# A second output row of the 3x3 convolution completed by accumulating transfers

## The chip, the cores and the metric

The kernel runs on one core of a Trainium2 chip. The metric is the device time of one execution in microseconds (us). Profiles are of one execution; a line L*n* is line *n* of the kernel before.

## The reference

Two bottleneck blocks follow each other on x of shape (64, 1024, 14, 14), float32. Each block is a 1x1 convolution to 256 channels, a 3x3 convolution from 256 to 256 channels with padding 1, and a 1x1 convolution back to 1024. Every convolution is followed by a batch normalization over images and pixels, and the first two also by a ReLU. The result is scaled by a softplus of one parameter, added to x and rectified:

```python
out = relu(bn(conv(x, w1, b1, 1, 0), g1, be1))
out = relu(bn(conv(out, w2, b2, 1, 1), g2, be2))
out = bn(conv(out, w3, b3, 1, 0), g3, be3)
return relu(x + softplus(residual_scale)[0] * out)
```

## The kernel before, in words

The 256 middle channels lie as two slots of 128 partitions in one tile `y` that stays in on-chip memory for the whole run. The stage of this change is the 3x3 convolution, `conv2`, once in each layer (from 305 to about 580 us and from 1276 to about 1560 us of the profile). It replaces `y` in place by the convolution of `y`, in eight groups `g` of eight images.

Along the rows a fast convolution with four output rows per tile and six products is used. For each group VectorE and ScalarE make six combinations of the input rows, in three pairs, (1, 2), (3, 4) and (5, 0) (`combine`). Products 3 and 4 have three row tiles (168 columns in a matmul), the others four (224). Each pair goes into tiles `r`, `v`, `sums` and `diffs` (`Inputs`). Along the columns there is a second fast scheme: TensorE makes for each product the parts `m` (from `sums`), `l` (from `diffs`) and `columns` (from `v`). ScalarE copies `m` into the two `columns` banks (L758, L760) and `l` to `ls` (L768). VectorE adds banks and `ls` into a tile `f` (L801, called from `outputs`). `f` has three buffers in turn, `columns` and `ls` two and three; the transformed filters of each product come by two loads on SP's queue (`ua`, `ub`, L651), which wait until TensorE has read the buffers.

`finish` turns the six products of a group, in the order in which they are made, into output rows. `out_rows[k]` are the rows k, k+4, ... of the 14. From the first two `f` it makes `a` and `d` (L829, L830: tiles `fa` and `fb` in the profile), from the next two `c` and `e` (L835, L836). Rows 1 and 2 are then written with L593 (the line of the helper `stt`). Row 0 lacks the sixth product, and row 3 and the last row (row 13, named `end`) lack the fifth. In the groups 0 to 5 (`by_transfer`) row 0 is begun by VectorE (L843) and ScalarE (L844), and completed by two transfers that add the sixth `f` to it (L871, GpSimd's queue). In the groups 6 and 7 VectorE completes it. Row 3 and `end` are completed by VectorE in all groups, in L859 and L860, from `d3` (the first three tiles of `d`, updated by L847 through the helper at L593) and the fifth `f`.

ScalarE also computes the statistics of the group before in four passes (`moment`, L900), which read all of that group's `y`, beside products 2 to 5 of a group, and normalizes the group that follows (`norm`) beside products 0 and 1.

On TensorE the order is written out in the loop at the end of `conv2`: `l` of product k, half of its `columns`, `m` of product k+1, the other half. On VectorE and ScalarE a scheduler orders the instructions, except where `keep_in_program_order` fixes them. All instructions of one engine start in order.

Of the kernel before, what the change touches and what calls it, by code (L numbers as in the profile page):

```python
# [38 lines left out]
AF = mybir.ActivationFunctionType  # L39
ALU = mybir.AluOpType  # L40

P = 128
N, C, H, W = 64, 1024, 14, 14
# [3 lines left out]
MS = M // P  # L47
# [40 lines left out]
def bottlenecks(ctx: ExitStack, tc: tile.TileContext, x, w1s, w2s, w3s, pars, out):  # L88
    nc = tc.nc
# [6 lines left out]
    y_grp = y_all.rearrange("p s (g h l) -> p s g h l", g=NG, h=H)  # L96
# [459 lines left out]
    def conv2(psum, pool, b, par, aff, affine_of, stats):  # L556
# [14 lines left out]
        full = RT - 1  # L571
# [12 lines left out]
        def new(tag, tiles=RT):  # L584
            v = pool.tile([P, MS * RT * LINE], FP, tag=tag, name=tag, bufs=BUFS.get(tag, 1))
            return v[:, : MS * tiles * LINE].rearrange("p (s r l) -> p s r l", s=MS, r=tiles)
# [5 lines left out]
        def stt(to, a, by, c):  # L592
            return nc.vector.scalar_tensor_tensor(to, a, by, c, ALU.mult, ALU.add)  # L593
# [210 lines left out]
        def halves(f):  # L804

            return f.rearrange("p o r (i q c) -> p q (o r i) c", i=GI, q=2)

        def outputs(c):
            return c.add_to(new("f", c.lines // GI))

        def finish():


            for g in range(NG):
                out_rows = [y_grp[:, :, g, k::4, :] for k in range(4)]
                last_group = g == NG - 1

                by_transfer = g < NG - 2

                def stat(k, lines):  # L820
                    if last_group:
                        for o in range(MS):
                            nc.vector.bn_stats(stats[:, o, 1 + k, :], lines[o])

                ca = yield
                fa = outputs(ca)
                fb = outputs((yield))
                a, d = new("fa"), new("fb")
                nc.vector.tensor_add(a, fa, fb)  # L829
                nc.vector.tensor_sub(d, fa, fb)  # L830

                fa = outputs((yield))
                fb = outputs((yield))
                c, e = new("fc", full), fa
                nc.vector.tensor_add(c, fa, fb)  # L835
                nc.vector.tensor_sub(e, fa, fb)  # L836
                a3, d3 = (v[:, :, :full] for v in (a, d))
                for o in range(MS):
                    stt(out_rows[1][:, o, :full], e[:, o], 2.0, d3[:, o])
                    stt(out_rows[2][:, o], c[:, o], 4.0, a3[:, o])  # L840
                if by_transfer:

                    nc.vector.tensor_add(out_rows[0][:, :, :full], a3, c)  # L843
                    nc.scalar.activation(out_rows[0][:, :, full], a[:, :, full], AF.Copy)  # L844
                else:
                    nc.vector.tensor_add(a3, a3, c)
                stt(d3, e, 8.0, d3)  # L847
                if g == 0:
                    begin(out_rows[1][:, :, :full])
                if last_group:  # L850
                    for o in range(MS):
                        lines = y_grp[:, o, g, 1 : 1 + 4 * full].rearrange("p (r k) l -> p r k l", k=4)[:, :, :2]
                        for k in range(2):
                            moment(lines, idle[:, : 2 * full * LINE].rearrange("p (r k l) -> p r k l", k=2, l=LINE), o, k, g)

                fa = outputs((yield))

                end = y_grp[:, :, g, H - 1]
                nc.vector.tensor_add(out_rows[3], d3, fa[:, :, :full])  # L859
                nc.vector.tensor_add(end, d[:, :, full], fa[:, :, full])  # L860
                stat(0, [out_rows[3][:, o] for o in range(MS)])
                stat(1, [end[:, o] for o in range(MS)])
                if last_group:
                    merge()

                cb = yield
                if by_transfer:

                    f = outputs(cb)
                    for o in range(MS):  # L870
                        nc.gpsimd.dma_start(out=out_rows[0][:, o], in_=f[:, o], accum_op=ALU.add)  # L871
                    continue
                nc.vector.tensor_add(halves(a), halves(a), cb.by_columns(cb.ls))
                for j, q in enumerate((EVEN, ODD)):
                    for o in range(MS):
                        to, more = (
                            v[:, o].rearrange("p r (i q c) -> p q r i c", i=GI, q=2)[:, q] for v in (out_rows[0], a)
                        )
                        nc.vector.tensor_add(to, cb.banks[:, q, o].rearrange("p (r i c) -> p r i c", r=RT, c=WH), more)
                    stat(2 + j, [out_rows[0][:, o].rearrange("p r (i q c) -> p q r i c", i=GI, q=2)[:, q] for o in range(MS)])  # L880
            yield
# [8 lines left out]
        def begin(lines):  # L890

            mv = small.tile([P, MS, nc.vector.BN_AGGR_DIM], FP, tag="mv_first", name="mv_first")
            for o in range(MS):
                nc.vector.bn_stats(first_stats[:, o], lines[:, o])
            for o in range(MS):
                nc.vector.bn_aggr(mv[:, o, :], first_stats[:, o])
            nc.vector.tensor_scalar(center, mv[:, :, 0], -1.0, None, ALU.mult)

        def moment(y, to, o, k, g):
            act(to, y, (AF.Identity, AF.Square)[k], bias=center[:, o : o + 1], accum_out=moments[:, o, k, g : g + 1])  # L900

        def merge():

            n = GPX * (NG - 1) + 2 * full * LINE
            m = small.tile([P, MS, 2], FP, tag="m12", name="m12")
            for o in range(MS):
                nc.vector.tensor_reduce(m[:, o], moments[:, o], mybir.AxisListType.X, ALU.add)
            eng = nc.gpsimd
            eng.tensor_scalar(m, m, 1.0 / n, None, ALU.mult)
            var = small.tile([P, MS], FP, tag="m12var", name="m12var")  # L910
            eng.tensor_tensor(var, m[:, :, 0], m[:, :, 0], ALU.mult)
            eng.tensor_sub(var, m[:, :, 1], var)
            eng.tensor_sub(m[:, :, 0], m[:, :, 0], center)

            for half in range(2):
                to = stats[:, :, 0, 3 * half : 3 * half + 3]
                eng.memset(to[:, :, 0], n / 2)
                eng.tensor_copy(to[:, :, 1], m[:, :, 0])
                eng.tensor_scalar(to[:, :, 2], var, n / 2, None, ALU.mult)
# [26 lines left out]


        made, finished = items(), finish()
        next(finished)
        queue = [next(made) for i in range(3)]  # L950
# [498 lines left out]
```

## Time and profile before

| what | value |
|---|---|
| median of 3 runs | 1959.65 us (1957.53 to 1960.48) |
| the profiled execution | 1959.24 us, span 1957.5 us |
| TensorE matmul / VectorE / ScalarE / GpSimd, busy share of the span | 98% / 79% / 53% / 27% |
| 3x3 convolution, 415 to 449 us (one group): PE / DVE / ACT / POOL busy | 33.67 / 33.35 / 24.98 / 2.55 us of 34.00 |
| DMA share there | 0.70 |
| L859, L860 (16 of each) | 847 and 381 ns |
| L871 (24) | 1262 to 1873 ns on GpSimd, 4.2 to 8.9 us to landing, median 6.5 |
| L844 (12) | 396 ns on ScalarE |

Busy times of VectorE and ScalarE overlap a little from one instruction to the next, so that in a dense stretch the start-to-start time is what counts (a VectorE instruction of 847 ns is followed after 770 ns). The DMA share is the mean busy share of 16 DMA engines.

### The profile page before, as it was taken

Reading aid. Unit: us, or ns where it says so; the run is one execution under the profiler, and the core shown is the slowest. Engines: PE = TensorE matmul, PEld = TensorE weight load, DVE = VectorE, ACT = ScalarE, POOL = GpSimd, SP = SyncE. Lnnn points to the kernel's source line nnn. Section 1 sums busy time; section 2 is a strip of 40 time slices with the busy share of each in tenths; the row PEclk is TensorE's granted clock in tenths of the full one; section 3 lists DMA queues with packets and bytes.
Section 4 is the critical chain, followed back from the end, with each engine's and each line's share of the span. In section 5 each row is a group of like instructions: output and inputs, shape, how many; then the busy total and the mean of one; then the engine's idle time right before and its main releaser. Section 6 shows DMA issues by size and latency. Waiting matters only on the chain.

```text
span 1957.5 us, 26989 instructions
## 1 busy us (share of the span) xinstructions
PE 1919.9 (98%) x9430; PEld 1614.4 (82%) x9430; DVE 1552.4 (79%) x2491; ACT 1041.5 (53%) x2082; POOL 532.0 (27%) x638
## 2 busy tenths in 40 slices
PE   9999999999999999999999999989999999999998
PEld 5555558999997799999999999989999887555554
DVE  5778768999998667676776776699999976888786
ACT  2222214677775055555555555457777641666665
POOL 0111100000105133433433333301010051666664
PEclk9999999999999999999999999999999999999999
DMA  7766635576747634444444444257667386899997
GB/s 289 278 248 254 249 112 165 178 208 191 207 142 203 198 135 187 173 165 177 182 169 165 179 184 166 99 183 204 203 192 207 124 199 232 298 322 339 336 341 264
DMA packets 188983, 408.39 MB, mean 209 GB/s; under 512 B 24944, under 2 KB 165136, under 8 KB 172336
## 3 DMA queue, kind: packets, MB, share of 16 engines
q1 hardware_dynamic: 161728, 324.66, 48.5%
q0 software_dynamic: 21504, 30.94, 6.9%
q10 hardware_dynamic: 5616, 51.06, 6.3%
q8 instruction: 75, 1.23, 0.3%
q14 instruction: 60, 0.49, 0.1%
HBM read 263.75 MB, written 115.34 MB: 194 GB/s over the span
## 4 chain that ended last, share of the span: by engine, by line
PE 90%; DVE 7%; issue 1%; ACT 1%; DMA 1%; SPq 0%; POOL 0%; DVEq 0%
PE ay L168 17%; PE cy L168 16%; PE columns L168 13%; PE cp L168 12%; PE ap L168 10%; PE m L168 6%; PE l L168 6%; PE ax L168 4%; PE cx L168 4%; PE ps L168 1%; DVE x L466 1%; DVE ct L431 1%; DVE f L801 0%; DMA home<-y 0%; DVE ct L433 0%
## 5 line engine op out<-in xcount | busy, mean ns | idle before, releaser
L333 ACT ACTIVATE cu<-cy,scale 128x196 f32<-128x196 f32 (+1 forms) x552 | 257.7, 473 | 286.7 <-PE cy L168 279.6
L168 PE MATMUL columns<-v,ub 128*128 128x224 f32 (+1 forms) x1536 | 301.1, 337 | 0.7 <-ACT columns L760 0.7
L168 PEld LDWEIGHTS columns<-v,ub 128*128 128x128 f32 x1536 | 269.4, 188 | 4.1 <-ACT columns L760 1.2
L333 ACT ACTIVATE x<-x,shift 128x392 f32<-128x392 f32 x428 | 239.7, 613 | 55.1 <-POOL x L492 53.2
L466 DVE SCALAR_TENSOR_TENSOR x<-cp,scale,x 128x196 f32<-128x196 f32 (+1 forms) x368 | 178.1, 484 | 98.0 <-PE cp L168 96.4
L168 PE MATMUL cy<-ct,ws 128*128 128x196 f32 (+1 forms) x736 | 222.0, 383 | 1.1 <-ACT cu L333 1.1
L168 PE MATMUL ay<-at,ws 128*128 128x196 f32 (+1 forms) x752 | 209.2, 381 | 0.0
L487 POOL TENSOR_TENSOR x<-x,cu 128x196 f32<-128x196 f32 (+1 forms) x184 | 159.2, 865 | 174.1 <-ACT cu L333 162.5
L492 POOL TENSOR_TENSOR x<-x,cu 128x392 f32<-128x392 f32 x124 | 125.9, 1015 | 192.8 <-DVE x L466 188.1
L168 PEld LDWEIGHTS ay<-at,ws 128*128 128x128 f32 x752 | 136.4, 190 | 33.6 <-ACT au L333 0.5
L168 PEld LDWEIGHTS cy<-ct,ws 128*128 128x128 f32 x736 | 133.4, 190 | 36.4 <-ACT cu L333 3.8
L168 PE MATMUL m<-sums,ua 128*128 128x224 f32 (+1 forms) x752 | 147.6, 340 | 6.2 <-DVE sums L624 6.2
L168 PE MATMUL l<-diffs,ub 128*128 128x224 f32 (+1 forms) x768 | 149.7, 338 | 3.0 <-PE columns L168 2.9
L513 POOL TENSOR_TENSOR x<-x,cu 128x392 f32<-128x392 f32 x120 | 124.5, 1038 | 86.1 <-DVE x L466 79.2
L871 POOL DMA_DIRECT2D y<-f x24 | 31.1, 1532 | 412.8 <-DVE f L801 320.8
L168 PEld LDWEIGHTS l<-diffs,ub 128*128 128x128 f32 x768 | 133.6, 189 | 7.0 <-PE columns L168 5.9
L168 PEld LDWEIGHTS m<-sums,ua 128*128 128x128 f32 x752 | 132.2, 191 | 8.7 <-DVE sums L624 7.9
L466 DVE SCALAR_TENSOR_TENSOR x<-cx,scale,x 128x196 f32<-128x196 f32 (+1 forms) x184 | 89.3, 485 | 59.1 <-PE cx L168 58.2
L333 ACT ACTIVATE au<-ay 128x196 f32<-128x196 f32 (+1 forms) x141 | 53.6, 380 | 152.0 <-PE ay L168 149.3
L168 PE MATMUL cx<-y,w 128*128 128x196 f32 (+1 forms) x404 | 124.1, 392 | 0.4 <-DVE x L1130 0.4
L168 PE MATMUL cy<-y,w 128*128 128x196 f32 (+1 forms) x404 | 123.8, 392 | 0.0
L168 PE MATMUL cp<-zt 128*128 128x257 f32 x392 | 118.8, 385 | 1.8 <-DVE zt L1030 1.7
(211 smaller groups left out, 3950.1 us busy)
## 6 DMA issues: line engine op xcount, KB each, us to landing
x<-in_x SPq DMA_DIRECT2D x62, 1568.0 KB, 6.8
ub<-u SPq DMA_DIRECT2D x94, 768.0 KB, 5.0
x<-mid SPq DMA_DIRECT2D x32, 1568.0 KB, 8.6
mid<-x ACTq DMA_DIRECT2D x31, 1568.0 KB, 5.1
out<-x SPq DMA_DIRECT2D x123, 392.0 KB, 6.5
ua<-u SPq DMA_DIRECT2D x94, 256.0 KB, 3.0
u<-y POOLq DMA_DIRECT2D x48, 256.0 KB, 5.9
home<-y SPq DMA_DIRECT2D x90, 96.0 KB, 4.2
```

The source lines that it names most:

```text
L168: tc.keep_in_program_order(nc.tensor.matmul(*args, **kw))
L333: tc.keep_in_program_order(nc.scalar.activation(*args, **kw))
L431: nc.vector.tensor_add(t2, t3, ys[0][0])
L466: nc.vector.scalar_tensor_tensor(v, bank, self.scale[:, o : o + 1], v, ALU.mult, ALU.add)
L487: nc.gpsimd.tensor_add(self.part(1, 1), self.part(1, 1), u3)
L492: nc.gpsimd.tensor_add(v, v, self.u12)
L513: nc.gpsimd.tensor_add(v, v, self.u12[:, i * self.n : (i + 1) * self.n])
L871: nc.gpsimd.dma_start(out=out_rows[0][:, o], in_=f[:, o], accum_op=ALU.add)
```

## The change

In the groups 0 to 5 of each layer, row 3 and `end` are completed by transfers with addition too. The update of `d3` now writes its result to row 3 of `y` instead of back to `d3`, in two instructions, one for each slot. ScalarE copies the last tile of `d` to `end`. When the fifth `f` is made, GpSimd's queue issues three transfers that add it to row 3 (one for each slot) and to `end`. L859 and L860 are run in the groups 6 and 7 alone.

```diff
-                stt(d3, e, 8.0, d3)
+                end = y_grp[:, :, g, H - 1]
+                if by_transfer:
+
+                    for o in range(MS):
+                        stt(out_rows[3][:, o], e[:, o], 8.0, d3[:, o])
+                    nc.scalar.activation(end, d[:, :, full], AF.Copy)
+                else:
+                    stt(d3, e, 8.0, d3)
...
                 fa = outputs((yield))
 
-                end = y_grp[:, :, g, H - 1]
-                nc.vector.tensor_add(out_rows[3], d3, fa[:, :, :full])
-                nc.vector.tensor_add(end, d[:, :, full], fa[:, :, full])
+                if by_transfer:
+                    for o in range(MS):
+                        nc.gpsimd.dma_start(out=out_rows[3][:, o], in_=fa[:, o, :full], accum_op=ALU.add)
+                    nc.gpsimd.dma_start(out=end, in_=fa[:, :, full], accum_op=ALU.add)
+                else:
+                    nc.vector.tensor_add(out_rows[3], d3, fa[:, :, :full])
+                    nc.vector.tensor_add(end, d[:, :, full], fa[:, :, full])
                 stat(0, [out_rows[3][:, o] for o in range(MS)])
```

## The prediction

> **What bounds the kernel now.** I read the page's busy shares first, then the busy time by stretch of one convolution group, then the instruction timeline of VectorE and TensorE at the changed place, then the waits.
>
> ```profile
> PE 1919.9 (98%) x9430; PEld 1614.4 (82%) x9430; DVE 1552.4 (79%) x2491; ACT 1041.5 (53%) x2082; POOL 532.0 (27%) x638
> ```
>
> ```profile
> 415.00:449.00 34.00, 33.67 (x194) 33.14 (x193) 33.35 (x37) 24.98 (x48) 2.55 (x2) 1.00 0.70 198
> ```
>
> The page says 79% for VectorE, an average over stages. In one group of the 3x3 convolution (second fence, the busy times by stretch; columns are stretch, length, busy us of PE, PEld, DVE, ACT, POOL, clock, DMA share, GB/s) VectorE is busy 33.35 of 34.00 us and TensorE 33.67. Both look full, so I ask which waits.
>
> ```profile
> 416.40 1.69 PE L168 MATMUL columns<-v,ub 128*128 128x224 f32 x8
> 418.42 1.75 PE L168 MATMUL l<-diffs,ub 128*128 128x224 f32 x8 [0.33 <-PE columns L168]
> ```
>
> ```profile
> 415.47 0.85 DVE L593 SCALAR_TENSOR_TENSOR fb<-f,fb 128x672 f32<-128x672 f32 x1
> 416.24 1.08 DVE L801 TENSOR_TENSOR f<-columns,ls 128x896 f32<-128x896 f32 x1
> 417.24 1.08 DVE L640 TENSOR_TENSOR diffs<-r 128x896 f32<-128x896 f32 x1
> 418.24 0.85 DVE L859 TENSOR_TENSOR y<-fb,f 128x672 f32<-128x672 f32 x1
> 419.01 0.38 DVE L860 TENSOR_TENSOR y<-fb,f 128x224 f32<-128x224 f32 x1
> 419.31 2.95 DVE L699 TENSOR_TENSOR steps<-y 128x2688 f32<-128x2688 f32 x1
> ```
>
> The first of these is TensorE's timeline, the second VectorE's (start, duration, engine, line). See that the block of eight matmuls at 416.40 is followed 2.02 us later, where its neighbours take 1.53: 0.49 us lost. The next block reads `diffs`, and VectorE finished `diffs` (L640) at 418.32. So TensorE waits for VectorE, once in a group. In the next groups the same instruction (L801 of the fifth product) starts 34.07 us later (450.31) and the `l` block 34.08 later (452.50), with the same loss. In another group the loss sits elsewhere:
>
> ```profile
> 468.96 1.30 PE L168 MATMUL l<-diffs,ub 128*128 128x168 f32 x8
> 470.59 1.42 PE L168 MATMUL columns<-v,ub 128*128 128x168 f32 x8 [0.33 <-ACT columns L760]
> ```
>
> ```profile
> 469.81 0.39 ACT L844 ACTIVATE y<-fa 128x224 f32<-128x224 f32 x1 [0.99 <-DVE fa L829]
> ```
>
> There ScalarE stood on L844, which waited for VectorE's `fa`, and the bank fill behind it came late: 1.63 us instead of 1.15, so 0.48 lost. The period is again 34.07. **VectorE's loop sets the period** (34.07, of which it idles only 0.30, for ScalarE's L715), TensorE needs 34.08 - 0.49 = **33.59**.
>
> **What the Trainium skill says.** *Trace Analysis* (Identifying the Most-Contended Engine) warns that matmul busy time doesn't tell how full TensorE is; the trace agrees: 98% busy, yet blocks stretch to 2.02 us. *DMA: Bandwidth & Descriptors* (SWDGE vs HWDGE vs iDMA) says that accumulating transfers go out from GpSimd alone, and that all issuing engines share 16 DMA engines; the trace shows L871 on the software queue, and a DMA share of 1.10 between 426 and 434 us, where they meet the filter loads. *SBUF — State Buffer* (Who interferes with whom) says that a two-input VectorE add meets only GpSimd reads of SBUF, not descriptor writing; the trace agrees: L593 and L624 keep 0.8 us each while L871 is issued (423.56 to 426.1). *VectorE: DVE Perf Modes* (TRN2 errata) says each VectorE instruction pays a fixed extra, so a split one costs more; here two 128x336 take 0.42 us each start to start, one 128x672 takes 0.77.
>
> **The change, part by part, for one of six groups in each of two layers.**
> VectorE: L859 (0.77 start to start) and L860 (0.30) go: -1.07. The update of `d3` (L847) becomes two halves: 2 x 0.42 - 0.77 = +0.07. Net **-1.00 us**. Its loop falls from 34.07 to about 33.07, below TensorE's 33.59, and TensorE becomes the bound: -0.48 a group. VectorE then runs ahead by about 0.5 us a group.
> ScalarE: one copy of 128x224 more (as L844: 0.30 start to start). ScalarE is busy 25 of 34 us; its copy reads `fb`, ready when L830 is done, well before the fifth product. Hidden by its 9 us of idle time.
> GpSimd: three issues more. L871's take 1.26 to 1.87 us, so about 4.2 us (bounds 3.8 to 5.6); the queue has 2.6 of 34 us busy. They start when the fifth `f` ends (417.32), are out by 421.5, and the sixth `f` ends at 423.26, so the old pair isn't delayed. Nothing else stands on that queue here.
> DMA engines: 384 + 384 + 256 rows of 448 bytes, as many as the pair of L871 (2 x 512). Between 345 and 520 us the software queue took 12.5% of 16 engines for 5280 packets: 66 ns each, 4.3 us per engine for 1024. The share rises from 0.70 to about 0.83. It falls at 418 to 427, where the share is 0.53 and 0.39 (416:422, 422:426), not on the 1.10 after it. SP's filter loads land in 5 us and are asked for two products (11 us) ahead: hidden, even 4.3 us later.
> New waits: the fifth `f` tile was free once L860 had read it. Now its buffer (three in turn) is free when the three transfers land. VectorE's second L801 of the next group takes it at 431.95, 14.6 us after 417.32. The third transfer is issued at 417.3 + 2 x 1.4 = 420.1; with the 6.5 us median of L871 it lands at 426.6, with its longest (8.9) at 429.0. Slack 3 to 5 us. Were it late, L829, L830 and all VectorE work for the next products would queue behind it, and then ScalarE's fills and TensorE. The moments (L900) wait for the same transfers, but read the rows at 435.12, behind the old pair.
> Order: in the built order of the changed kernel, VectorE's `diffs` for the next products stands ahead of the `e`/`y` work, so the wait at 418.42 loses its cause; in four of six groups L844 stands between the two bank fills, the order that lost 0.48 at 470.59. With VectorE ahead by over 0.5 us that wait is covered after one or two groups. TensorE's and SP's orders are unchanged.
>
> **The sum.** Start-to-start excess of TensorE's blocks from the fifth product of group 0 on. Layer 0: 0.50, 0.49, 0.48, 0.45 in the groups changed, 0.49 and 0.64 in the last two. Layer 1: 0.65, 0.30, 0.50, 0.49, 0.44, then 0.73 and 0.74. Changed groups 4.3, last two groups 2.6, together 6.9 us. The two stalls of 2.78 us in group 0 (TensorE waits for `sums`, done before L859 starts) stay, as does 1.6 us at half clock in layer 0. The last two groups keep their VectorE work; five groups x 0.5 us of lead help them, and I take two thirds, 1.7. So -4.3 - 1.7 = **-6.0 us**. The profiled execution took 1959.24 (span 1957.5, 1.7 around it), 0.4 under the median of 1959.65. 1959.24 - 6.0 = **1953.2 us**. All of it would give 1952.3, half 1955.8.
>
> **Rivals.**
> A, the wait is only exchanged: L844 between the fills, or a later `f`, costs TensorE 0.48 in each of eight groups in which VectorE isn't ahead. Then 6.9 - 8 x 0.48 = 3.1 remain: 1956.1. For it: that order lost 0.48 in this trace. Against: it lost it with a VectorE loop of 34.07, and that loop is now 33.07.
> B, **slower: the transfers hold the `f` buffer.** If the third lands later than the 14.6 us, VectorE waits at its second L801 for the excess, twelve times; the 1.00 us saved in its loop pays for the first part. With landings of 15 us from issue (435.1) VectorE waits 3.1 us, its loop is 33.07 + 3.1 = 36.2, and the kernel 12 x 2.1 = 25 us slower: 1984. It decides from a landing 13 us after issue. For it: small rows, a queue shared with 55% of filter loads, five accumulating transfers in a row where there were two. Against: L871's longest landing is 8.9 us, and the new ones fall in the emptier stretch.
> C, nothing gained: TensorE's 33.59 hides a limit of the same size (ScalarE's fills), 1959. Against: ScalarE idles 9 us a group.
>
> **How the numbers follow.** About 0.2% (3.9 us) is what a measurement of this kernel can tell from no change. Forecast 0.70 (1951.5 to 1955.5), A 0.13, C 0.05, B 0.12 (1965 to 1990). Of A a third still passes 0.2%. So faster 0.74, same 0.14, slower 0.12. The range takes in forecast and A and leaves out B and most of C: 1951 to 1958.5.
>
> **What would show it.** Right: L859 and L860 only four times each; TensorE blocks at 1.53 with no 2.02 in the middle groups; period of a group 33.6; VectorE busy about 32.3 of 33.6 with idle time in front of L801 or L593; new transfers landing in 6 to 9 us; DMA share about 0.83. Wrong: VectorE idle in front of L801 put down to DMA, ScalarE waiting at the moments for DMA, TensorE waits on ACT L760 in most groups, or a period still at 34.1.

## The result and the profile after

The changed kernel takes 1952.45 us (median of 6 runs, 1949.66 to 1952.98), the kernel before 1958.63 us (6 runs, 1957.53 to 1960.48). The medians are 6.2 us apart. The recorded ratio is 0.9963 with a 95% interval of 0.9952 to 0.9974, which is 5 to 9 us: a small gain and a real one. Measured once more beside the kernel before (e10 below) the medians were 7.6 us apart and the ratio was 0.9961 (0.9949 to 0.9974). The profiled execution has a span of 1951.0 us, where before had 1957.5.

Profiles of a changed kernel show its own line numbers, which are those of before up to L846. In the changed kernel L867 is the pair of transfers to row 3, L868 the one to the last row, L882 the old pair to row 0 (L871 before), and L852 ScalarE's new copy.

The page's busy shares of the changed kernel hardly move:

```profile
PE 1918.5 (98%) x9430; PEld 1617.1 (83%) x9430; DVE 1541.4 (79%) x2479; ACT 1044.6 (54%) x2094; POOL 577.1 (30%) x674
```

VectorE has lost 11.0 us of busy time and the run 6.5 us of span. GpSimd has 45 us more busy time, and nothing waits for it. The stretch of one group shows the change of regime (stretch, length, busy us of PE, PEld, DVE, ACT, POOL, clock, DMA share, GB/s):

```profile
415.00:448.60 33.60, 33.60 (x194) 33.38 (x194) 32.93 (x37) 25.27 (x49) 6.37 (x5) 1.00 0.83 216
```

TensorE is now busy in all 33.60 us. VectorE has 0.7 us to spare. The DMA share rose from 0.70 to 0.83. Next TensorE's and VectorE's timelines at the changed place of the changed kernel (start, duration, engine, line):

```profile
416.34 1.69 PE L168 MATMUL columns<-v,ub 128*128 128x224 f32 x8
417.87 1.67 PE L168 MATMUL l<-diffs,ub 128*128 128x224 f32 x8
419.38 1.69 PE L168 MATMUL columns<-v,ub 128*128 128x224 f32 x8
```

```profile
415.62 1.08 DVE L801 TENSOR_TENSOR f<-columns,ls 128x896 f32<-128x896 f32 x1
416.62 2.95 DVE L699 TENSOR_TENSOR steps<-y 128x2688 f32<-128x2688 f32 x1
419.48 1.08 DVE L801 TENSOR_TENSOR f<-columns,ls 128x896 f32<-128x896 f32 x1
```

The block that took 2.02 us takes 1.53. Behind the fifth product's L801 the two additions are gone, L699 follows at once. `diffs`, for which TensorE had waited, stands earlier (410.56, not shown); e3 below tells whether this new order makes the gain. The waits of TensorE from 336 to 555 us say the same, first of before, then of the changed kernel (who waited for whom, us in total, times, longest):

```profile
PE m L168 <- DVE sums L624: 2.6, 1, 2.6
PE l L168 <- PE columns L168: 1.2, 4, 0.3
PE columns L168 <- ACT columns L760: 0.3, 1, 0.3
```

```profile
PE m L168 <- DVE sums L624: 2.7, 1, 2.7
```

One wait is left, in group 0, ahead of the new transfers (2.69 us where it was 2.61). VectorE's waits in the same stretch of the changed kernel name no DMA:

```profile
DVE r L593 <- ACT r L715: 3.2, 6, 0.7
DVE f L801 <- PE columns L168: 1.0, 1, 1.0
DVE r L682 <- DVE steps L593: 0.5, 1, 0.5
```

Most of VectorE's spare time comes out as a longer wait for ScalarE's L715, which it already had (1.8 us in the same stretch of before). GpSimd's timeline of the changed kernel shows the five issues of a group:

```profile
417.00 2.57 POOL L867 DMA_DIRECT2D y<-f  x2 [26.75 <-DVE f L801]
418.88 1.92 POOL L868 DMA_DIRECT2D y<-f  x1
420.87 2.57 POOL L882 DMA_DIRECT2D y<-f  x2
```

They leave no gap. The DMA view of 345 to 520 us gives the software queue's share and the median time to landing (KB each, us):

```profile
q0 software_dynamic: 10881, 4.70, 23.9%
...
y<-f POOLq DMA_DIRECT2D x10, 224.0 KB, 7.5
y<-f POOLq DMA_DIRECT2D x12, 168.0 KB, 4.6
y<-f POOLq DMA_DIRECT2D x6, 112.0 KB, 8.0
```

The smallest transfer, to the last row, takes longest to land (8.0): it is the third in line. In e4 below the same transfer is issued alone, and lands in 4.0 us (median). Issued at 418.88 it lands at about 426.9; its `f` is taken by L801 at 430.26. 3.4 us of cover are left.

### The profile page after: what moved, and what is told of

Its sections match the earlier page's. It is cut to its first block, busy times and chain, and to the rows that moved or that the text cites. A ratio compares the mean times of both kernels' runs of the same rounds, so it can differ in the third digit from the quotient of the medians.

```text
span 1951.0 us, 27071 instructions
## 1 busy us (share of the span) xinstructions
PE 1918.5 (98%) x9430; PEld 1617.1 (83%) x9430; DVE 1541.4 (79%) x2479; ACT 1044.6 (54%) x2094; POOL 577.1 (30%) x674
## 4 chain that ended last, share of the span: by engine, by line
PE 88%; DVE 5%; issue 5%; ACT 1%; POOL 1%; DMA 1%; SPq 0%; DVEq 0%; POOLq 0%; ACTq 0%
PE cy L168 16%; PE columns L168 14%; PE ay L168 14%; PE cp L168 12%; PE ap L168 9%; PE l L168 7%; PE m L168 7%; PE cx L168 4%; PE ax L168 4%; PE ps L168 1%; DVE x L466 1%; POOL u L215 1%; DVE ct L431 1%; DMA u<-y 0%; DVE ct L433 0%
## 5 line engine op out<-in xcount | busy, mean ns | idle before, releaser
L867 POOL DMA_DIRECT2D y<-f x24 | 30.9, 1529 | 349.5 <-DVE f L801 309.0
```

The lines of the kernel that those rows point to most:

```text
L867: nc.gpsimd.dma_start(out=out_rows[3][:, o], in_=fa[:, o, :full], accum_op=ALU.add)
```

## The experiments

The theory is that VectorE's loop per group sets the period as long as it exceeds TensorE's own need, 33.5 us, and that beyond this point less VectorE work gains nothing. The rivals are a gain that comes from the new order of VectorE's instructions or from other waits, a gain in proportion to the work removed, and a hidden price of the transfers.

**e1, VectorE's additions kept beside the transfers.**

```diff
                     nc.gpsimd.dma_start(out=end, in_=fa[:, :, full], accum_op=ALU.add)
+                    nc.vector.tensor_add(d3, d3, fa[:, :, :full])
+                    nc.vector.tensor_add(d[:, :, full], d[:, :, full], fa[:, :, full])
```

> The changed kernel with its three transfers, and with VectorE's two additions of the same shapes as before (128x672 and 128x224) kept beside them, in groups 0 to 5. Their results go to tile d and are not used: they cost VectorE 1.07 us a group, and nothing else is changed. The scheduler puts VectorE's order back to that of before. Theory (VectorE's loop sets the period): the loop is 34.07 + 0.07 = 34.14 us again, all of the gain is lost, 1958.6 to 1960 us. Rival 1 (the gain is from the transfers taking the rows out of some wait, not from VectorE's time): it stays at 1952.5. Rival 2 (transfers cost something that the gain hid): over 1961.

Measured: 1959.28 us beside 1959.25 of before, ratio 1.0 (0.9992 to 1.0009). All of the gain is gone with VectorE's time restored. A hidden price of the transfers would show here as a time above that of before: they are all there, and the interval allows 1.8 us at most. VectorE's order is that of before too, so that e1 alone doesn't part its time from its order.

**e2, the new transfers left out.**

```diff
                 if by_transfer:
-                    for o in range(MS):
-                        nc.gpsimd.dma_start(out=out_rows[3][:, o], in_=fa[:, o, :full], accum_op=ALU.add)
-                    nc.gpsimd.dma_start(out=end, in_=fa[:, :, full], accum_op=ALU.add)
+                    pass
```

> The changed kernel without its three new transfers a group: the fifth product is left out of row 3 and the last row in groups 0 to 5; VectorE's and ScalarE's work is that of the changed kernel. Theory: the transfers are hidden, so the time is that of the changed kernel, 1952.4 within 1 us. Rival 1 (the transfers cost TensorE or VectorE something that the gain covered): faster, 1950 or less.

Measured: 1951.42 us, ratio 0.996 (0.9948 to 0.9973). The change has 0.9963 and 0.9961 with nearly the same intervals. The profiles say it more sharply: the stage (from its first matmul to the matmuls that follow its last product) takes 278.64 and 277.54 us in the two layers of e2, and 278.68 and 277.55 us in those of the change in e10. The transfers are hidden.

**e3, row 3 alone, and e4, the last row alone.** In e3:

```diff
-                    nc.scalar.activation(end, d[:, :, full], AF.Copy)
...
-                    nc.gpsimd.dma_start(out=end, in_=fa[:, :, full], accum_op=ALU.add)
+                    nc.vector.tensor_add(end, d[:, :, full], fa[:, :, full])
```

> Row 3 alone goes by transfer in groups 0 to 5 (two transfers), VectorE completes the last row as before (128x224, 0.30 us start to start), ScalarE's copy is left out. Theory (two bounds, VectorE's loop and TensorE's 33.59): VectorE's loop is 34.07 - 0.77 + 0.07 = 33.37, still below 33.59, so the changed groups gain all (4.3 us) and the last two a part, for the lead is only 0.2 us a group: 1952.5 to 1954.5. Rival (gain in proportion to VectorE's work removed, 0.70 of 1.00 us): 1954.3 or more, with stalls left on TensorE in the middle groups.

Measured: 1951.22 us, ratio 0.9963 (0.9951 to 0.9976). It is about as fast as the whole change with 0.70 of its 1.00 us removed, and faster than the 1952.5 to 1954.5 that was expected, for TensorE's stalls in the last two groups went too. TensorE keeps two small losses, 0.56 us in a group of layer 0 and 0.19 in one of layer 1. In the group at 414 us VectorE makes `diffs` (415.15) behind the fifth product's L801 (414.15), in the order of before, and TensorE's `l` block starts on time (416.69, 1.53 us after the block ahead of it). So the gain doesn't need the new order. In e4:

```diff
-                    for o in range(MS):
-                        stt(out_rows[3][:, o], e[:, o], 8.0, d3[:, o])
+                    stt(d3, e, 8.0, d3)
...
-                    for o in range(MS):
-                        nc.gpsimd.dma_start(out=out_rows[3][:, o], in_=fa[:, o, :full], accum_op=ALU.add)
+                    nc.vector.tensor_add(out_rows[3], d3, fa[:, :, :full])
```

> The last row alone goes by transfer in groups 0 to 5 (one transfer, ScalarE's copy kept), VectorE completes row 3 as before in one 128x672 addition. Theory: VectorE's loop is 34.07 - 0.30 = 33.77, still over TensorE's 33.59, so VectorE stays the bound; the period falls by 0.30 to 33.77 and TensorE keeps a stall of about 0.2 us a group: 1954.5 to 1956.5. Rival (any of the new waits or the order does it): either 1952.5 or 1958.6.

Measured: 1956.24 us, ratio 0.9987 (0.9981 to 0.9994), 3.0 us below the kernel before. Here too `diffs` stands behind the fifth product's L801 (415.29 and 414.29). The periods tell why e4 lies between. L699 runs once a group on VectorE; the distance of its starts is the period. From the timelines of before, e1, e4, e3 and the changed kernel, in this order:

```profile
419.31 2.95 DVE L699 TENSOR_TENSOR steps<-y 128x2688 f32<-128x2688 f32 x1
453.38 2.95 DVE L699 TENSOR_TENSOR steps<-y 128x2688 f32<-128x2688 f32 x1
```

```profile
453.57 2.95 DVE L699 TENSOR_TENSOR steps<-y 128x2688 f32<-128x2688 f32 x1
487.71 2.95 DVE L699 TENSOR_TENSOR steps<-y 128x2688 f32<-128x2688 f32 x1
```

```profile
450.83 2.94 DVE L699 TENSOR_TENSOR steps<-y 128x2688 f32<-128x2688 f32 x1
484.60 2.94 DVE L699 TENSOR_TENSOR steps<-y 128x2688 f32<-128x2688 f32 x1
```

```profile
483.16 2.95 DVE L699 TENSOR_TENSOR steps<-y 128x2688 f32<-128x2688 f32 x1
516.65 2.95 DVE L699 TENSOR_TENSOR steps<-y 128x2688 f32<-128x2688 f32 x1
```

```profile
483.27 2.95 DVE L699 TENSOR_TENSOR steps<-y 128x2688 f32<-128x2688 f32 x1
516.78 2.96 DVE L699 TENSOR_TENSOR steps<-y 128x2688 f32<-128x2688 f32 x1
```

| kernel | VectorE's loop as worked out beforehand | period shown |
|---|---|---|
| before | 34.07 (measured) | 34.07 |
| e1, additions kept | 34.14 | 34.14 |
| e4, last row alone | 33.77 | 33.77 |
| e3, row 3 alone | 33.37 | 33.49 |
| the change | 33.07 | 33.51 |

Down to 33.77 the period follows VectorE's sum to 0.01 us. Below it stops at about 33.5, which is TensorE's. The two last pairs are from groups in which VectorE has its lead; before that it makes up its delay of group 0, at 33.2 us a group in the changed kernel. TensorE keeps one distance all along there: its `l` block of 417.87 comes again 33.51 us later,

```profile
451.38 1.68 PE L168 MATMUL l<-diffs,ub 128*128 128x224 f32 x8
```

and from the end of group 0 on its groups follow each other at 33.51 us (to 0.02) in both layers. Nothing that VectorE still has to spare can shorten that. Against a gain in proportion speaks e3's trace: 0.75 us of loss are left on TensorE, where before had some 8.3 and a gain in proportion would have left 2.5. Its interval alone reaches 1954.5 us and wouldn't exclude that rival (1954.3).

**e5 and e6, two buffers for `f` in place of three,** in the changed kernel and in the kernel before:

```diff
-BUFS = dict(ua=3, ub=3, sums=2, diffs=2, v=2, ls=3, f=3)
+BUFS = dict(ua=3, ub=3, sums=2, diffs=2, v=2, ls=3, f=2)
```

> The changed kernel with two buffers for f in place of three (BUFS f=2). In the changed kernel's trace the third of the new transfers is issued at 418.9 and lands about 8 us later, at 426.8; with two buffers its f is taken by the first L801 of the next group (425.9), no longer by the second. Theory (three buffers are the cover of the landing): VectorE waits about 1 us a group at that L801, its loop is about 34.1, and the gain is lost: 1957 to 1961, with VectorE's wait put down to DMA. Rival (the landing has more slack than that): 1952.5.

Measured: 1956.98 us, ratio 0.9992 (0.9984 to 1.0), 4.5 above the change's median; single runs spread from 1953.3 to 1962.3. VectorE's timeline and ScalarE's behind it in e5:

```profile
392.21 1.09 DVE L801 TENSOR_TENSOR f<-columns,ls 128x896 f32<-128x896 f32 x1 [1.81 <-DMA y<-f]
397.69 1.09 DVE L801 TENSOR_TENSOR f<-columns,ls 128x896 f32<-128x896 f32 x1 [0.66 <-DMA y<-f]
```

```profile
401.49 0.39 ACT L844 ACTIVATE y<-fa 128x224 f32<-128x224 f32 x1 [2.17 <-DVE fa L829]
```

This is the chain that the prediction's slower rival described: VectorE waits for landings at L801, `fa` comes late, ScalarE stands on L844 between two bank fills, and TensorE's block behind it starts 1.7 us late. It occurs here in some groups. With two buffers the first of these L801 takes the buffer of the fifth `f`, which the new transfers read, and the second that of the sixth, which the old pair reads. In all, VectorE waits 4.7 us in three places for the new transfer to the last row and 3.1 us in four for the old pair.

> The kernel before with two buffers for f. Its fifth f is read by VectorE alone, and its sixth is free when the two transfers of row 0 land, at about 432, when the second L801 of the next group takes it (431.95). Theory: at most some tenths of a us a group, 1958.5 to 1962. Rival (two buffers cost by themselves, for L829 and L830 have to be done before the third f): clearly slower, over 1963, and then the run before this one says nothing of landings.

Measured: 1965.63 us, ratio 1.0035 (1.0022 to 1.0049). That is 6.4 us in the kernel before without a new transfer, and over what was expected. The waits of VectorE in layer 1 (1300 to 1545 us) have a line that the kernel before lacks:

```profile
DVE f L801 <- DMA y<-f: 2.9, 3, 1.7
```

With two buffers the landing of the old pair alone is too late, in three groups of layer 1. In this profile the stage is 0.6 us longer in layer 0 and 4.6 in layer 1; of the latter, these waits are 2.9 and a spell at half clock (see the end of this document), which before had in layer 0 alone, is 1.7. So the rival's reason for a loss, that L829 and L830 have to be done before the third `f`, isn't what the trace shows. By its waits, e5's loss is one of landings too, of the new and of the old transfers; how much each costs the two runs don't part. Beside e6, e5 is 8.7 us faster: with two buffers the change gains no less than with three.

**e7, the first statistics later.** The wait left in group 0 is for `sums`, which stand on VectorE behind the rows of group 0 and behind `begin`:

```diff
-                if g == 0:
-                    begin(out_rows[1][:, :, :full])
...
                 fa = outputs((yield))
+                if g == 0:
+                    begin(out_rows[1][:, :, :full])
```

> The changed kernel, with the first statistics (begin, L894 to L897, about 1.2 us of VectorE) called after the fifth f of group 0. They stand ahead of the sums for which TensorE waits 2.8 us in group 0 of each layer. Theory: TensorE's wait falls to about 1.6 us in each layer, 2.4 us in all, 1950; more, up to 1947, if the shorter gap spares the half clock that follows it in some executions. Rival (the wait moves to the diffs that follow): 1952.5.

Measured: 1948.97 us, ratio 0.9944 (0.9932 to 0.9957). TensorE's loss there (its excess over the usual time of a block) fell from 2.86 to 1.83 us in each layer, and another 0.53 appeared ahead of the next `l` block. That is 1.0 us less in both layers together. The two stages are 1.9 us shorter than in e10's profile, in which a spell at half clock that cost 1.5 us followed this wait; in e7's profile there is none.

**e8, all of group 0's rows later.** The writing of rows 0 to 3 and `begin` go into a function `rows_out`, the three new transfers into `row_3`:

```diff
+                if g:
+                    rows_out()
                 fa = outputs((yield))
...
                 cb = yield
+                if g == 0:
+                    rows_out()
+                    row_3()
```

> The changed kernel, with all of group 0's writing of rows 0 to 3 and its first statistics (about 4.7 us of VectorE) put behind the sums and diffs of the next group's first pair; its new transfers follow them. Theory: TensorE's wait of 2.8 us in group 0 goes, 5.7 us in both layers, less what the postponed work costs later (VectorE's lead is only 0.5 us a group): 1946.5 to 1950. Rival (the postponed work stops TensorE one or two products later, for ScalarE's bank fills wait for the sixth f): 1951 to 1954.

Measured: **1946.95 us**, ratio 0.9935 (0.9922 to 0.9947), 4.6 us below the change in e10 and the fastest version tried. Its runs lie within 0.3 us, those of the change within 3.3 at first and 1.1 in e10. TensorE's waits from 336 to 555 us in e8:

```profile
PE m L168 <- DVE sums L624: 0.6, 2, 0.4
PE l L168 <- PE columns L168: 0.4, 1, 0.4
```

Of 2.85 us in group 0, 1.6 remain as three losses of 0.4 to 0.6 us between 353 and 381 us: the postponed work, not wholly taken in. As in e7, there is no half clock.

**e9, the same with row 3 alone by transfer, and e10, the change once more beside it.**

> The kernel with group 0's rows written later, with row 3 alone completed by transfer (the last row by VectorE as before, one transfer and one ScalarE copy less a group). Theory: VectorE's loop of 33.37 us is still below TensorE's, so it is not slower than with all three transfers, 1946 to 1948; its smaller lead (0.1 to 0.2 us a group) may leave a stall behind the postponed work, up to 2 us. Rival (the lead is needed to take in the postponed work): 1949 or more.

Measured: 1950.23 us, ratio 0.9953 (0.9939 to 0.9966). The rival's number came: alone, row 3 gave nearly all of the gain, but with work postponed it is 3.3 us slower than e8. TensorE's losses behind group 0 are 0.95, 0.34 and 0.88 us (0.59, 0.39 and 0.58 in e8), and one of 0.49 stays in the middle. The two stages are 2.4 us longer than in e8. This fits the rival's reason, that the lead takes in the postponed work; the lead itself wasn't varied in any other way.

> The changed kernel as it is, beside the run before this one on the same chip, to set row 3 alone against the whole change. Expected 1952.4, within 1 us.

Measured: 1951.56 us, ratio 0.9961 (0.9949 to 0.9974).

**e11, group 0's rows later in the kernel before.** The edit of e8 without the change: VectorE keeps L859 and L860.

> The kernel before (VectorE completes row 3 and the last row), with group 0's rows and first statistics written later, as in the run e8. Theory (VectorE's loop is the bound there): VectorE's work is all kept, so the 2.8 us that TensorE no longer waits in group 0 are waited for in the following groups; what can be gained is VectorE's own idle time in group 0 (1.35 us in layer 0, none in layer 1) and the half clock: 1956.5 to 1959.5. Rival (the wait in group 0 adds to the time whatever VectorE does later): 5.5 us faster, 1953.5, as much as the same edit gave on top of the change.

Measured: 1957.52 us, ratio 0.999 (0.9982 to 0.9998), 1.5 us gained where the same edit gave 4.6 on top of the change. TensorE's waits of e11, 336 to 555 us:

```profile
PE m L168 <- DVE sums L624: 1.5, 1, 1.5
PE l L168 <- issue: 1.5, 1, 1.5
PE l L168 <- PE columns L168: 0.6, 2, 0.3
PE columns L168 <- ACT columns L760: 0.3, 1, 0.3
```

The wait in group 0 is gone, and losses of 1.66 and 1.64 us come at 354 and 381 us, as well as the half-microsecond ones of the middle groups. With VectorE as the bound, a TensorE wait that goes comes back further on. Both gains contain a spell at half clock that went with the wait: the two stages are shorter by 2.2 us in e11 than in before, by 3.7 in e8 than in e10, and 1.6 and 1.5 of that are the half clock.

## Why the prediction was right

The forecast was 1953.2 us, 6.0 less than before; 1952.45 and 6.2 less were measured, and 7.6 less in e10. The mechanism is the one forecast. That the number fits so closely is partly luck: TensorE gained more than was summed, and in the profiled execution the clock took a part of it back. By its steps:

- **The bound.** That VectorE's loop sets the period, and TensorE's need once VectorE's loop is shorter, is shown by e1, e4 and e3, from both sides.
- **VectorE, -1.00 us a group.** e4's 33.77 and e1's 34.14 come out of the same start-to-start times (0.77, 0.30, 2 x 0.42). With all of the change, VectorE's shortest distance is 33.2, 0.1 more than the 33.07 worked out; it doesn't count, as TensorE is the bound there.
- **TensorE's need, 33.59.** Too high by 0.08: it is 33.51. Beside the wait, the block behind it was longer too (1.59 us, from 418.42 to 420.01, where such blocks take 1.51), and this was not counted as loss.
- **The sum, -4.3 and two thirds of 2.6.** All of the 6.9 us went: from the fifth product of group 0 on, no block with an excess of the listed kind is left, not in the last two groups either. With the longer blocks behind the waits, and waits too short for the list, some 8.3 went. In the profile of e10 the stage is shorter by 3.92 us in layer 0 and 4.37 in layer 1, 8.3 together.
- **The half clock.** In the profile of the change the clock fell after the wait in group 0 in both layers (excess 1.8 and 1.6 us), in that of before in layer 0 alone (1.6). That takes some 1.8 us back in this execution and explains why its stages gained 3.63 and 2.69. The sum had assumed that it stays as it was. Whether it explains the 6.2 us between the medians isn't shown, for the other runs have no profile.
- **Transfers.** 13 points of DMA share, 3.8 us of issue a group (4.2 worked out) and no wait. One step was off: the end of the sixth `f` was put at 423.26, but VectorE now ends it at 420.56, so the old pair follows at 420.87 without a gap, and DMA is crowded at 422 to 426 (share 1.35), not spread. The old pair lands in 7.5 us (median) where 6.5 were measured before. Nothing waits for it.
- **Rival A (the wait exchanged).** L844 does stand between the fills and ScalarE waits for `fa`, 1.5 us in four groups of layer 0; the `columns` block behind it starts on time. In e3, where VectorE's lead is smaller, this order did cost TensorE 0.44 us once (433.08).
- **Rival B (slower by landings)** didn't decide: the landing was 8 us, and 3.4 us of cover were left. e5 and e6 show its mechanism at work with one buffer less.

## What to carry to other kernels

When two engines are both over 98% busy in a stage, work out the period of each from start-to-start times and look which one waits: the smaller relief (0.70 us a group) was worth nearly as much as the larger, for the gain ends where the second engine's period begins. Work taken off the bound by accumulating transfers was free here while their landing had time to spare (e2), and no longer with one buffer less (e5), so count that time before and after. Once the bound has moved, look again at old stalls: the same reordering gave 1.5 us before the change and 4.6 after it.

## What the runs showed of the hardware that was not expected

A TensorE gap of 2.6 to 2.7 us was followed by 3.4 us at half clock in some cases and not in others, in the same place of the same kernel (in layer 1 of the change, but not in that of e10). The nine profiles with this gap in group 0 have it in 10 of 18 layers; where it came, the half clock lasted 3.4 us each time and cost TensorE 1.5 to 1.8 us. One stretch of it, in layer 0 of the change (columns as above; the clock is the third number from the end):

```profile
347.00:348.00 1.00, 1.00 (x4) 0.92 (x3) 1.00 (x2) 0.00 (x0) 1.00 (x2) 0.50 1.10 111
```

With the gap cut to 1.66 us (e7) it wasn't seen in either layer. What decides whether it comes the runs don't show.

And a transfer's place and company in the queue counted for more than its bytes. GpSimd took longer to issue the transfer to the last row (L868, 112 KB, 1.92 to 2.29 us) than those to row 3 (L867, 168 KB, 1.25 to 1.84); the issues overlap, for L868 begins at 418.88 and the second L867 ends at 419.57. In e4 the transfer to the last row is issued alone (its L866), with the same shape, and takes 1.17 to 1.26 us to issue and 4.0 to land (median; 7.9 as the third of three):

```profile
L866 POOL DMA_DIRECT2D y<-f x12: 1171/1185/1257, 345.1 to 1486.2; - x12
```
